# A long convolution fused with a 4-bit gated feed-forward: the last group's kernel tables move from a burst into the first down stage

## The chip, the core and the metric

The kernel runs on one core of a Trainium2 chip. The metric is device time in microseconds (us) of one launch; lower is better. Engines are named as in the profile: PE (TensorE matmul), PEld (its weight loads), DVE (VectorE), ACT (ScalarE), POOL (GpSimd), SP (SyncE, here used only to issue DMAs).

## The reference

`x` is 32 x 64 x 1024 (batch, channel or head, time). Every head is convolved along time with a kernel of 1024 taps made from 64 complex exponentials, and masked by a length for each batch row; the result goes through a feed-forward over the time axis whose weights are 4-bit with a scale and a zero point for each group of 128 rows; `x` is added.

```python
K = 2.0 * einsum('hn,hnl->hl', Cs, exp(P)).real      # P = dtA * arange(L), complex
y = (irfft(rfft(u_m, 2L) * rfft(K, 2L))[..., :L] + u_m * D[:, None]) * mask
gate, up = y2 @ Wg, y2 @ Wu                           # 1024 -> 2752, dequantized in groups of 128
out = x + ((gate * sigmoid(gate) * up) @ Wd)          # 2752 -> 1024
```

## The kernel before

The 64 heads make four blocks of 16 heads; a block is 16 x 32 = 512 columns. The convolution of a head is a product with a Toeplitz matrix: `conv_head` loads it from a padded kernel in DRAM (`t <- kpad`, L525, 512 KB, three buffers `t0`), runs 24 small matmuls (L548) in eight steps of three, and after every second head masks the result on DVE (`y`, L560) and splits it into a high and a low fp16 half (`xh` on ACT, L563; `xl` on POOL, L565). The results of a block fill a pair of tiles `x[b]`, 8 x 512 columns each: blocks 0 and 2 in `x[0]`, blocks 1 and 3 in `x[1]`. The input `u` of four heads is loaded at a time (L503) and split by ACT (L507) and DVE (L510).

The taps of a head's kernel come from tables, made for eight heads at a time: decays (POOL product L175, Exp on ACT L179), phases (DVE L192 to L204), Sin and Square on ACT (L207, L209), factors on DVE (L218 to L223), a small product `kq` on PE (L425, L427), its split `kb` (ACT L430, DVE L431) and two stores to `kpad` (L433). The Toeplitz loads of these heads follow the stores.

The feed-forward runs in chains. A chain has one PSUM buffer and runs over the groups of 128 rows: four matmuls of 512 columns, then one rescale of the PSUM tile by a ratio of scales, on DVE or on ACT, before the next group may add to it. Up chains (`gu_one`, `gu_pair`) have eight groups (matmuls L687, L688; rescales L618 on DVE, L620 on ACT; Silu L695, product L700). Down chains (`dn_pair`) have 21 groups and a rest: matmuls L736 and L737, rescales L637 on DVE and L640 on ACT, the rest `ic` in L741; they end with `o` (L754 DVE or L758 ACT), two additions to the residual `xr` (L762, one on POOL, one on DVE) and two stores. The residual, 512 KB of `x`, is loaded by SP (L775).

The stages, in order, four chains to each down stage:

| stage | chains | beside them |
|---|---|---|
| 0, 1, 2 | up, blocks 0 and 1 | convolution of block 1, unpacking of weights, tables of heads 32 to 47 |
| 3 | down, block 0 | unpacking of down weights (`unpack_it`), `fourth_it`, `convs_it` |
| 4 | down, block 1 | `fourth_it`, `convs_it` |
| 5 | up, blocks 2 and 3 | |
| 6, 7 | down, blocks 2 and 3 | residuals of block 3 |

`fourth` makes the tables of heads 48 to 63 in two groups of eight; `convs` runs the convolution of blocks 2 and 3. `x[0]` and `x[1]` are free from the end of stage 2 until a convolution fills them again.

The order is made by a planner, `roll`. It steps three (in stages 3 and 4) or four open chains in turn, one group each. After each of these steps it makes a *side step*: every side job of the stage gets credit by its rate in `RATES` and runs as many of its own steps as it has credit for. A job with `None` also needs `c.room()`: by the planner's own clocks for PE, DVE and ACT, DVE may be at most 1.2 us ahead of PE and ACT 1.5 us, or it waits; it saves up at most two credits. `convs_it` needs no room. The job marked `True` (`convs_it` in stage 4) is run to its end when the first chain of the next stage opens, which is when the second chain of the stage ends; `c.forced` is set then, and with it all pauses are skipped. A down chain of block 1 follows the last chain of block 0 by two groups or more, since it waits for loads that that chain releases.

The calls become engine queues through the tile framework's scheduler, which takes ready instructions by their place in the program; `with self.after("dve")` ties the instructions inside behind the last rescale issued on that engine.

Unpacking a piece of the weights uses a tile `z` of zero points from a pool `up` with four buffers (`c.up_stack`, right side of SBUF): two loads (L578, L579), a shift on DVE (L584), two additions on POOL that read `z` (L590), two casts on DVE (L599). The steps of the unpacking have pauses for the landing of the loads. Before the change `fourth` waits until all of the down weights are unpacked, closes `up`, and opens a pool `kg2` in that memory for its small tiles. The residual tiles of blocks 0 to 2 share the two buffers of tag `sg` with the Silu results. `convs` forces what is left of the unpacking and of `fourth` between its two blocks:

```python
    def convs():
        yield from c.conv(2)
        c.forced = True
        c.need(*(("dn", k, part) for k in range(4) for part in range(3)))
        every(fourth_it)
        c.forced = False
        yield from c.conv(3)
```

Of the kernel before, what the change touches and what calls it, by code (L numbers as in the profile page):

```python
# [9 lines left out]
F32 = mybir.dt.float32  # L10
# [19 lines left out]
KSCALE = 64.0  # L30
PLACES = {("a", "pair"): 1, ("a", "single"): 2, ("b", "pair"): 3}
MAGIC = 12582912.0
RATES = {"first": (0.5, 4.6), "fill": (1.0, 0.8), "third": 0.5, "convs": 1.9}
HOP, MM, LANDING = 220.0, 215.7, 6000.0
LAG, HEAD_STARTS = 2, [4, 2, 1]
DVE_ROOM, ACT_ROOM = 1200.0, 1500.0
# [190 lines left out]
class Later:  # L227
    def __init__(self, make, *args):
        self.make, self.args, self.gen = make, args, None
# [18 lines left out]
def every(gen):  # L248
    for _ in gen:
        pass  # L250
# [8 lines left out]
class Core:  # L259
    def __init__(self, ctx, tc, io):  # L260
        self.tc, self.nc, self.io = tc, tc.nc, io
        pool = lambda name, **k: ctx.enter_context(tc.tile_pool(name=name, **k))
        self.keep = pool("keep", bufs=1)
        self.cv = pool("cv", bufs=2)
        self.fw = pool("fw", bufs=2)
        self.up_stack = ctx.enter_context(ExitStack())
        self.up = self.up_stack.enter_context(tc.tile_pool(name="up", bufs=4, side="right"))
        self.dram = pool("dram", bufs=1, space=DRAM)
        self.ps, self.ps_stack, self.ps_mode = {}, {}, {}
        for place in "ba":  # L270
            self.ps_stack[place] = ctx.enter_context(ExitStack())
            self.banks(place, "single" if place == "a" else "pair")
        self.tp = self.td = self.ta = 0.0
        self.forced = True
        self.bank_free = {"a": [], "b": []}
        self.kpad = self.dram.tile([H, 2, 1152], F16, name="kpad")
        self.dm, self.known, self.ready = {}, set(), set()
        self.marks = {}
        self.sg, self.t0, self.us, self.raw = {}, {}, {}, {}
        self.passed, self.loaded, self.fac = {}, {}, {}  # L280
        keep = self.keep
        self.w = keep.tile([128, NI, 2, GH, 128], F8, name="w")
        self.wmix = keep.tile([128, GH, 128], F8, name="wmix")
        self.x = [[keep.tile([128, 8, 512], F16, name=f"x{k}{b}") for k in "hl"] for b in range(2)]
        self.ihl = keep.tile([128, 21, 2, 512], F16, name="ihl")
        self.ic = [keep.tile([128, 512], F16, name=f"ic{b}") for b in range(2)]
        self.spill = self.dram.tile([21, 128, 2, 512], F16, name="spill")
        self.zc = self.dram.tile([128, ZBYTES // 128], U8, name="zc")
# [429 lines left out]
    def dn_pair(self, k, blk, place):  # L718
        nc = self.nc
        apart = self.ps_mode[place] == "single"  # L720
        if apart:
            qs = [self.psum("chq", place)[:, 0] for _ in range(2)]
        else:
            q = self.psum("chq", place)
            qs = [q[:, j] for j in range(2)]
        ready = [self.bank(place)] * 2
        for g in range(GI):
            while blk % 2 == 1 and g < 21 and not self.loaded.get((blk, min(20, g + LAG))):
                yield
            if g in (0, 8, 16):  # L730
                self.need(("dn", k, g // 8))
            for j in range(2):
                self.pe((2 if g < 21 else 1) * MM, ready[j])
                lw = self.wd[k][:, g, 128 * j:128 * j + 128]
                if g < 21:
                    nc.tensor.matmul(qs[j], lw, self.ihl[:, g, 0], start=(g == 0), stop=False, skip_group_check=True)  # L736
                    nc.tensor.matmul(qs[j], lw, self.ihl[:, g, 1], start=False, stop=False, skip_group_check=True)  # L737
                    if apart:
                        ready[j] = self.rescale_bank(qs[j], self.rdn[:, 2 * k + j, g:g + 1])
                else:  # L740
                    nc.tensor.matmul(qs[j], lw, self.ic[blk % 2], start=False, stop=True, skip_group_check=True)  # L741
            if g < 21:
                if not apart:
                    ready = [self.rescale_two(q, self.rdn[:, 2 * k:2 * k + 2, g:g + 1])] * 2
                self.passed[blk, g] = self.passed.get((blk, g), 0) + 1
                if blk % 2 == 0 and self.passed[blk, g] == 4:
                    nc.scalar.dma_start(self.ihl[:, g], self.spill[g])
                    self.loaded[blk + 1, g] = True
                yield
        xr = self.res[k] if blk == 3 else self.residual(self.fw, 2 * k, blk)  # L750
        take = self.last_o if blk == 3 else lambda shape, dt: self.fw.tile(shape, dt, name="o", bufs=2)
        o = take([128, 2, 512], F16)
        if not apart and self.on_dve(1240, 1380):
            nc.vector.tensor_tensor(o, q, self.ldn[:, 2 * k:2 * k + 2].unsqueeze(2).to_broadcast([128, 2, 512]), ALU.mult)  # L754
            free = self.dve(1240, self.tp + HOP)
        else:
            for j in range(2):
                nc.scalar.activation(o[:, j], qs[j], AF.Copy, scale=self.ldn[:, 2 * k + j:2 * k + j + 1])  # L758
                free = self.act(690, self.tp + HOP)
        for j in range(2):  # L760
            n = 2 * k + j
            (nc.vector if j == 1 else nc.gpsimd).tensor_tensor(xr[:, j], xr[:, j], o[:, j], ALU.add)  # L762
            if blk < 3:
                store = nc.gpsimd
            else:
                store = nc.scalar if apart and j == 1 else nc.sync
            store.dma_start(self.io["out"][128 * n:128 * n + 128, 512 * blk:512 * blk + 512], xr[:, j])
        self.dve(1000)
        self.bank_free[place].append(free + HOP)
        yield  # L770

    def residual(self, pool, n0, blk):
        rows, cols = slice(128 * n0, 128 * n0 + 256), slice(512 * blk, 512 * blk + 512)
        xr = pool([128, 2, 512], F32) if callable(pool) else pool.tile([128, 2, 512], F32, name="xr", tag="sg", bufs=2)
        self.nc.sync.dma_start(  # L775
            xr, self.io["xT"].rearrange("l h b -> l (h b)")[rows, cols].rearrange("(k p) t -> p k t", p=128))
        return xr
# [65 lines left out]
def tile_ssm_ffn(ctx, tc, io):  # L843
    nc = tc.nc
    c = Core(ctx, tc, io)
# [141 lines left out]
    third_it = third()  # L987
# [13 lines left out]
        return make  # L1001

    def fourth():
        c.forced = True
        every(third_it)
        c.forced = False
        while not c.ready.issuperset(("dn", k, part) for k in range(4) for part in range(3)):
            yield
        c.up_stack.close()
        with tc.tile_pool(name="kg2", bufs=1, side="right") as kg2:  # L1010
            space = c.x[1]
            yield from c.decays(c.scratch(space[:1]), (48, 56))
            c.taps(kg2, 48)
            for h0 in (48, 56):
                yield from c.tables(ScratchPool(c.scratch(space[1:])), h0, 8)
                yield from c.factors(kg2, h0, 8, c.xds[h0])
                for _ in range(3):
                    yield
                c.make_kernel(kg2, h0, 8, "a")
                yield  # L1020

    fourth_it = fourth()

    def convs():
        yield from c.conv(2)
        c.forced = True
        c.need(*(("dn", k, part) for k in range(4) for part in range(3)))
        every(fourth_it)
        c.forced = False
        yield from c.conv(3)  # L1030

    def residuals():
        take = c.scratch(c.x[0])
        c.res = [c.residual(take, n0, 3) for n0 in (0, 2, 4, 6)]
        c.last_o = c.scratch(c.x[1])
        yield

    convs_it = convs()
    second_it = second()
    sides = {  # L1040
        0: [(unpack_it, RATES["first"][0], None), (group_it, 1.0, None), (second_it, RATES["first"][1], True)],
        1: [(unpack_it, RATES["fill"][0], None), (third_it, RATES["fill"][1], None)],
        2: [(third_it, RATES["third"], None), (unpack_it, RATES["fill"][0], None)],
        3: [(unpack_it, RATES["fill"][0], None), (fourth_it, RATES["fill"][1], None), (convs_it, RATES["convs"], False)],
        4: [(fourth_it, RATES["fill"][1], None), (convs_it, RATES["convs"], True)],
        6: [(residuals(), 1.0, True)],
# [80 lines left out]
```

## Time and profile before

| | |
|---|---|
| median of 3 runs | 1074.47 us (1073.33 to 1075.77) |
| the profiled execution | 1075.33 us, its span 1073.5 us |
| PE busy | 1026.2 us, 96% of the span |
| DVE busy | 803.7 us, 75% |
| ACT busy | 775.6 us, 72% |
| POOL busy | 246.5 us, 23% |
| mean granted PE clock | 0.992 |
| down matmuls of stages 3 and 4 | from 395.2 us |
| convolution of block 3 | 510.5 to 580.3 us |

Busy PE time is from modelled ends of pipelined matmuls: it shows where PE waits, not how near it is to its peak. A matmul of 512 columns shows 380 ns but a new one starts every 0.216 us when nothing holds PE. The granted clock is the share of full speed that PE was given; it is read beside the idle time, since matmuls at half clock still count as busy.

### The profile page before, as it was taken

How to read it: one execution, taken by the hardware profiler on the slowest of the kernel's cores; microseconds unless marked ns; L12 is line 12 of the kernel's file. 1: busy time of each engine (PE TensorE's matmuls, PEld its weight loads, DVE VectorE, ACT ScalarE, POOL GpSimd, SP SyncE). 2: the span in 40 equal slices, each digit the busy share in tenths (PEclk: the TensorE clock that was granted, in tenths of full speed). 3: DMA queues.
4: the chain of work that ended last, by engine and by line, in shares of the span. 5: the costliest groups of instructions: out<-in, count | busy, mean ns of one | idle time of the engine just before them, and what ended most of it. 6: DMA issues, size and time to landing. Idle time of an engine off the chain costs nothing.

```text
span 1073.5 us, 15382 instructions
## 1 busy us (share of the span) xinstructions
PE 1026.2 (96%) x5854; PEld 513.5 (48%) x5854; DVE 803.7 (75%) x939; ACT 775.6 (72%) x1034; POOL 246.5 (23%) x270
## 2 busy tenths in 40 slices
PE   3989999999999999997999999999999999999996
PEld 2867444444344445663665444444444444444442
DVE  8965788888977786768446777777877777777776
ACT  5767777787677777777577777666666667878775
POOL 0333233232332242231103112221111222102102
PEclk9999999999999999999999999999999999999998
DMA  6976321111111534546753001000000001424102
GB/s 197 331 244 211 101 69 40 40 59 40 42 48 50 143 88 156 164 156 196 231 167 128 30 29 51 20 13 17 20 20 20 20 20 58 129 79 148 59 1 79
DMA packets 52099, 99.76 MB, mean 93 GB/s; under 512 B 9524, under 2 KB 11444, under 8 KB 52024
## 3 DMA queue, kind: packets, MB, share of 16 engines
q1 hardware_dynamic: 38888, 70.09, 20.8%
q0 software_dynamic: 5280, 17.31, 4.3%
q10 hardware_dynamic: 7856, 11.37, 3.6%
q8 instruction: 46, 0.75, 0.3%
q14 instruction: 29, 0.24, 0.1%
HBM read 78.99 MB, written 19.76 MB: 92 GB/s over the span
## 4 chain that ended last, share of the span: by engine, by line
PE 83%; ACT 5%; DMA 4%; DVE 4%; issue 2%; POOL 0%; SPq 0%; DVEq 0%; ACTq 0%
PE chq L687 23%; PE chq L688 22%; PE chq L736 13%; PE chq L737 13%; PE cq L548 6%; PE chq L664 2%; PE chq L665 2%; DMA t<-kpad 2%; ACT chq L640 1%; DVE chq L618 1%; ACT chq L620 1%; DVE v L700 1%; DMA ihl<-kpad 1%; DMA ihl<-xF 1%; PE chq L741 1%
## 5 line engine op out<-in xcount | busy, mean ns | idle before, releaser
L687 PE MATMUL chq<-xh,w 128*128 128x512 f16 x1216 | 460.4, 380 | 5.7 <-DVE chq L618 2.1
L688 PE MATMUL chq<-xl,w 128*128 128x512 f16 x1216 | 458.6, 380 | 0.0
L618 DVE TENSOR_SCALAR chq<-chq,gur 128x1024 f32<-128x1024 f32 x261 | 333.2, 1289 | 95.3 <-PE chq L688 94.1
L620 ACT ACTIVATE chq<-chq,gur 128x1024 f32<-128x1024 f32 x285 | 304.3, 1085 | 86.8 <-PE chq L688 85.5
L640 ACT ACTIVATE chq<-chq,dnr 128x512 f32<-128x512 f32 x372 | 242.1, 661 | 71.7 <-PE chq L737 63.8
L736 PE MATMUL chq<-ihl,wd 128*128 128x512 f16 x672 | 253.8, 380 | 6.5 <-ACT chq L640 3.5
L737 PE MATMUL chq<-ihl,wd 128*128 128x512 f16 x672 | 253.4, 380 | 0.0
L637 DVE TENSOR_TENSOR chq<-chq,dnr 128x1024 f32<-128x1024 f32 x129 | 158.4, 1231 | 83.6 <-PE chq L737 83.2
L688 PEld LDWEIGHTS <-w 128*128 128x128 fp8e4 x1216 | 118.9, 98 | 155.3 <-issue 19.4
L687 PEld LDWEIGHTS <-w 128*128 128x128 fp8e4 x1216 | 118.9, 98 | 145.9 <-issue 1.9
L310 POOL TENSOR_TENSOR ihl<-v,ihl 128x512 f16<-128x512 f32 x42 | 48.3, 1150 | 362.9 <-ACT ihl L629 362.9
L737 PEld LDWEIGHTS <-wd 128*128 128x128 fp8e4 x672 | 65.5, 98 | 76.0 <-issue 12.7
L548 PEld LDWEIGHTS <-t 128*128 128x128 f16 x1152 | 81.4, 98 | 39.2 <-DMA t<-kpad 5.9
L736 PEld LDWEIGHTS <-wd 128*128 128x128 fp8e4 x672 | 65.7, 98 | 67.7 <-issue 1.7
L548 PE MATMUL cq<-uh,t 128*128 128x256 f16 (+3 forms) x720 | 91.8, 226 | 4.6 <-DMA t<-kpad 4.5
L565 POOL TENSOR_TENSOR xl<-y,xh 128x512 f16<-128x512 f32 x28 | 36.2, 1294 | 161.5 <-ACT xh L563 161.5
L548 PE MATMUL cq<-ul,t 128*128 128x256 f16 (+3 forms) x360 | 71.6, 225 | 0.0
L629 ACT CAST ihl<-v 128x512 f16<-128x512 f32 x42 | 25.9, 617 | 58.7 <-DVE v L700 55.3
L700 DVE SCALAR_TENSOR_TENSOR v<-chq,gul,sg 128x1024 f32<-128x1024 f32 x38 | 48.6, 1280 | 17.1 <-PE chq L688 11.3
L310 POOL TENSOR_TENSOR spill<-v,spill 128x512 f16<-128x512 f32 x42 | 48.8, 1161 | 14.2 <-ACT spill L629 13.9
L640 ACT ACTIVATE chq<-chq,gur 128x512 f32<-128x512 f32 x66 | 43.2, 661 | 11.0 <-PE chq L665 9.8
L590 POOL TENSOR_TENSOR w<-w,z 128x256 int32<-128x256 int32 x42 | 31.5, 770 | 82.0 <-DVE w L584 77.6
(250 smaller groups left out, 820.5 us busy)
## 6 DMA issues: line engine op xcount, KB each, us to landing
t<-kpad SPq DMA_DIRECT2D x48, 512.0 KB, 4.4
spill<-spill POOLq DMA_DIRECT2D x42, 256.0 KB, 2.7
ihl<-spill ACTq DMA_DIRECT2D x42, 256.0 KB, 2.8
z<-zc SPq DMA_DIRECT2D x29, 256.0 KB, 3.7
u<-xF SPq DMA_DIRECT2D x12, 512.0 KB, 3.7
xr<-xT SPq DMA_DIRECT2D x12, 512.0 KB, 4.7
out<-xr POOLq DMA_DIRECT2D x24, 256.0 KB, 2.9
w<-qgu SPq DMA_DIRECT2D x21, 256.0 KB, 4.1
```

Of the source, the lines that this page charges most:

```text
L310: self.nc.gpsimd.tensor_tensor(out, a, b, op)
L548: nc.tensor.matmul(q[:, d:, h % 2, :], t0[:, lw, 128 * d:128 * d + 128], uu[:, 0:8 - d, h % 4, :], start=(d == 0 and k == 0 and h % 2 == 0 ...
L565: split.tensor_tensor(xl[:, :, ts], yv, xh[:, :, ts], ALU.subtract)
L618: self.mark("dve", self.nc.vector.tensor_scalar(q, q, col, None, ALU.mult))
L620: self.mark("act", self.nc.scalar.activation(q, q, AF.Copy, scale=col))
L637: self.mark("dve", self.nc.vector.tensor_tensor(q, q, cols.to_broadcast([128, 2, 512]), ALU.mult))
L640: self.mark("act", self.nc.scalar.activation(q[:, k], q[:, k], AF.Copy, scale=cols[:, k]))
L687: nc.tensor.matmul(q[:, b], lw, xh[:, g, :], start=(g == 0), stop=False, skip_group_check=True)
L688: nc.tensor.matmul(q[:, b], lw, xl[:, g, :], start=False, stop=(g == GH - 1), skip_group_check=True)
L700: nc.vector.scalar_tensor_tensor(v, q, last, self.sg.pop(ct - 21), ALU.mult, ALU.mult)
L736: nc.tensor.matmul(qs[j], lw, self.ihl[:, g, 0], start=(g == 0), stop=False, skip_group_check=True)
L737: nc.tensor.matmul(qs[j], lw, self.ihl[:, g, 1], start=False, stop=False, skip_group_check=True)
```

## The change

- `fourth` no longer waits for the unpacking, and no longer uses `kg2`. From the start of stage 3 it takes all of its memory from `x[1]`: decays in the first half of the high tile, the dpad row, factors and `kb` in the rest of it and the last eighth of the low tile, phase tables in the other seven eighths.
- Between the factors and `make_kernel` it pauses until the planner's PE clock has reached its DVE clock, in place of three steps.
- `convs` no longer forces anything between its blocks. If heads 56 to 63 are not known it lets its steps pass; only when it is itself run to the end does it run `fourth` on.
- The rate of `convs` goes from 1.9 to 1.52 steps for each side step.
- The residuals of blocks 0 to 2 get a pool `xrp` of two buffers in the memory of `up`. The first down chain to end forces what is left of the unpacking, closes `up` and opens `xrp`.

```diff
-RATES = {"first": (0.5, 4.6), "fill": (1.0, 0.8), "third": 0.5, "convs": 1.9}
+RATES = {"first": (0.5, 4.6), "fill": (1.0, 0.8), "third": 0.5, "convs": 1.52}
...
-        xr = self.res[k] if blk == 3 else self.residual(self.fw, 2 * k, blk)
+        if blk == 3:
+            xr = self.res[k]
+        else:
+            if self.xrp is None:
+                self.need(*(("dn", j, part) for j in range(4) for part in range(3)))
+                self.up_stack.close()
+                self.xrp = self.up_stack.enter_context(self.tc.tile_pool(name="xrp", bufs=2, side="right"))
+            xr = self.residual(self.xrp, 2 * k, blk)
...
-        xr = pool([128, 2, 512], F32) if callable(pool) else pool.tile([128, 2, 512], F32, name="xr", tag="sg", bufs=2)
+        xr = pool([128, 2, 512], F32) if callable(pool) else pool.tile([128, 2, 512], F32, name="xr")
...
     def fourth():
-        c.forced = True
-        every(third_it)
-        c.forced = False
-        while not c.ready.issuperset(("dn", k, part) for k in range(4) for part in range(3)):
+        first, second = c.x[1]
+        yield from c.decays(c.scratch([first[:, :4]]), (48, 56))
+        c.taps(ScratchPool(c.scratch([first[:, 4:6]])), 48)
+        for h0 in (48, 56):
+            small = ScratchPool(c.scratch([first[:, 6:8], second[:, 7:8]]))
+            yield from c.tables(ScratchPool(c.scratch([second[:, :7]])), h0, 8)
+            yield from c.factors(small, h0, 8, c.xds[h0])
+            yield from c.pause(c.td - c.tp + HOP)
+            c.make_kernel(small, h0, 8, "a")
             yield
-        c.up_stack.close()
-        with tc.tile_pool(name="kg2", bufs=1, side="right") as kg2:
-            space = c.x[1]
-            yield from c.decays(c.scratch(space[:1]), (48, 56))
-            c.taps(kg2, 48)
-            for h0 in (48, 56):
-                yield from c.tables(ScratchPool(c.scratch(space[1:])), h0, 8)
-                yield from c.factors(kg2, h0, 8, c.xds[h0])
-                for _ in range(3):
-                    yield
-                c.make_kernel(kg2, h0, 8, "a")
-                yield
...
     def convs():
         yield from c.conv(2)
-        c.forced = True
-        c.need(*(("dn", k, part) for k in range(4) for part in range(3)))
-        every(fourth_it)
-        c.forced = False
+        while 56 not in c.known:
+            if c.forced:
+                next(fourth_it)
+            yield
         yield from c.conv(3)
```

More of the change, by code (lines that the diff above doesn't have):

```diff
@@ L276, in __init__ @@
         self.kpad = self.dram.tile([H, 2, 1152], F16, name="kpad")
+        self.xrp = None
         self.dm, self.known, self.ready = {}, set(), set()
```

## The prediction, made before the changed kernel ran

> **What bounds the kernel now.** I read the page's forty slices first, then the windows of 10 us, then inside the weak stretch the chain of waits and PE's timeline.
>
> ```profile
> PE   3989999999999999997999999999999999999996
> PEclk9999999999999999999999999999999999999998
> ```
>
> One slice is 26.8 us. PE is full from the fourth slice to the last but one, with a single "7", at 483 to 510 us. Whatever does not touch PE's gaps there moves little. The windows show the hole (columns: stretch, length, busy us of PE, PEld, DVE, ACT, POOL with counts, granted clock, DMA share, GB/s):
>
> ```profile
> 480.00:490.00 10.00, 9.99 (x74) 5.33 (x73) 8.23 (x10) 7.10 (x10) 6.24 (x7) 1.00 0.78 266
> 490.00:500.00 10.00, 6.36 (x36) 2.74 (x35) 9.85 (x21) 7.08 (x12) 0.00 (x0) 0.86 0.54 178
> 500.00:510.00 10.00, 7.25 (x43) 2.97 (x42) 7.33 (x12) 7.80 (x16) 0.00 (x0) 0.97 0.56 156
> 510.00:520.00 10.00, 8.53 (x98) 6.75 (x99) 1.31 (x3) 3.21 (x6) 1.15 (x1) 1.00 0.92 297
> 520.00:530.00 10.00, 10.00 (x79) 6.04 (x78) 6.44 (x6) 7.07 (x11) 1.16 (x1) 1.00 0.51 161
> 497.00:500.00 3.00, 3.00 (x23) 1.43 (x22) 3.00 (x7) 1.22 (x2) 0.00 (x0) 0.53 0.31 87
> ```
>
> PE idles 3.64 + 2.75 + 1.47 us; DVE has 21 instructions in the first of the three; from 497 to 500 us the clock is 0.53. The chain of waits says what PE waited for (start, length, what):
>
> ```profile
> 491.24 1.24 ACT chq L640 x2
> 492.50 1.28 ACT L207
> 493.79 0.94 ACT xl L207 x2
> 494.73 0.82 ACT xl L209 x2
> 495.55 1.14 ACT chq L640 x2
> ...
> 504.58 5.92 DMA t<-kpad
> 510.55 1.71 PE cq L548 x24
> 512.27 4.72 DMA t<-kpad
> ```
>
> First a down chain's rescale (L640) stands behind the sine tables (L207, L209) of the last group of heads, all issued in one burst. Then the first Toeplitz loads (t<-kpad) of block 3 start only when that burst has written its kernel to DRAM.
>
> How much is lost: from 484 to 518 us PE ran 34 matmuls each on L736 and L737, at the unhindered spacing of 0.216 us: 14.7 us. The convolution pieces in the chain and timeline add up to 6.1 us (three heads from 510.55 to 515.39, and ends), the kq matmuls to 2.7 us. That is 23.5 us of work in 34 us: **10.5 us lost**, 7.9 of it idle, some 1.4 (3.0 x 0.47) half clock, the rest small seams.
>
> A page differs on the clock: by the Trainium skill, "TensorE: Matmul & The Clock Gate", section "What's actually happening", the clock halves only after about 3.4 us idle. The longest gap here was 2.21 us, so by that rule 1.4 us less would be recoverable; the row decides.
>
> **The change, part by part.**
>
> *The burst becomes a side job (saves up to 10.5 us).* The last group's tables no longer wait for the last unpacking and are no longer forced in one go. The instructions stay the same. On DVE a group has 14 (L192 0.68, L194 0.68, L197 0.48, L198 0.34, L200 0.68, L201 0.41, L203 0.74, L204 0.47, five of about 0.41 in L218 to L223, L431 0.41): 7.0 us, two groups 13.9 us. On ACT: two table loads of 1.28, Exp 1.06, sines and squares 1.86 and 2.02, two kb of 0.37: 8.2 us. They go into the stretch 406 to 484 us, where DVE was busy 52.1 of 78 us and ACT 57.9. Each goes to about 66 of 78, 85%; with the slower convolution pace the same chain work takes some 74 us, so near 90%. That cover is thin. The nearest row is the same job done earlier for heads 32 to 47 inside the up stage:
>
> ```profile
> 220.00:230.00 10.00, 9.78 (x45) 4.28 (x44) 7.32 (x7) 9.69 (x11) 4.77 (x6) 1.00 0.18 66
> 230.00:240.00 10.00, 9.51 (x44) 4.13 (x43) 10.00 (x15) 7.30 (x10) 1.95 (x3) 1.00 0.29 79
> 240.00:250.00 10.00, 9.83 (x47) 4.33 (x46) 9.77 (x10) 5.46 (x7) 0.92 (x1) 1.00 0.00 0
> 250.00:260.00 10.00, 9.19 (x42) 3.90 (x41) 7.75 (x11) 8.15 (x10) 5.21 (x6) 1.00 0.15 55
> 280.00:290.00 10.00, 8.00 (x29) 3.00 (x28) 9.39 (x10) 4.81 (x6) 6.58 (x8) 0.83 0.15 54
> ```
>
> There PE lost 1.7 us over 40 us, and once, at 280 us, 2.0 idle plus 1.7 (10 x 0.17) of clock. Bounds 0 to 5.4 us; I take 2.0, next to the 1.7.
>
> The two table switches now delay rescales in a stage that needs ACT. In the trace a switch costs its 1.28 us and the next ACTIVATE starts 0.01 us later (492.50 to 493.79). "ScalarE: Activation LUTs", section "What ACT_TABLE_LOAD costs", in the Trainium skill speaks against the move: it counts a drain too, 2.66 us a switch. By it ACT would have 2.8 us more; no such drain shows here.
>
> Of what else moves with it: the dpad load and the four kpad stores (16 KB) pass on SP ahead of Toeplitz loads of block 2. Two of them held SP 2.25 us at 508.72; those loads are issued up to three heads (about 14 us) ahead, so 0. The two POOL multiplies of the decays were already hoisted to 385 and 392 us and waited there 7.6 us for the up stage; they write the same half of the same block: 0. Behind them on POOL stand only unpacking adds.
>
> *The convolution pace, 1.9 to 1.52.* Blocks 2 and 3 are 32 heads of 8 steps, 256. Stage 5 opens when the second chain of stage 4 ends, its last matmul at 576.17 us, and what remains is drained at once:
>
> ```profile
> 576.00:582.00 6.00, 2.45 (x33) 2.10 (x32) 1.00 0.09 35
> ```
>
> That is L548 alone: 33 matmuls, 11 steps left; 245 were done, so 245 / 1.9 = 129 side steps. At 1.52 they give 196: **60 steps, 7.5 heads, will be drained in one block** at stage 5's door. PE's work is the same, and the first five sixths of stages 3 and 4 get shorter by what is put off. What a block costs is the wait for Toeplitz loads: three buffers, a load issued at 512.27 landed 4.72 us later, while two further heads last 3.2 us. At 515.39 this left 1.65 us, half filled by chain matmuls: PE idled 0.84. Behind the first three heads come 4.5 more, 1.5 such gaps, 2.5 us unfilled, 1.3 at that filling. Two chains of stage 4 are at hand to fill. Bounds 0 to 4.5 (unfilled, with one half-clock stretch of 2 us); I take 1.5.
>
> Whether the tables are ready in time: block 2 needs 128 / 1.52 = 84 side steps. The new generator takes about 5 + 3 steps for the decays and 16 for each group (pauses counted at 1.1 us a step), 40 in all; at rate 0.8 that is 50 side steps if DVE and ACT have room, and there are 84 before block 3 would wait and 129 before stage 5.
>
> *Residuals in the unpacking's memory.* Two buffers as before, but loads for the first two chains can't start at 400 us any more; they wait for the last POOL add of the unpacking (465.7 us). Chain ends were at 472.0 and 478.9, a load lands in about 4.7 us: just in time, as the third chain's was already (issued 480.86, added 484.77, no wait). If late, DVE would hold rescales behind its add (L762). Bounds 0 to 2 x 4.7; I take 0.5. The forced end of the unpacking pulls forward at most three DVE instructions (0.41 + 0.68 + 0.78), which ended at 472.4 anyway: 0, at worst 1.9. In stage 5 and 6 silu tiles no longer share buffers with residuals; the seam at 640 us (9.91 of 10) says 0.1 at most.
>
> **Sum.** 10.5 - 2.0 - 1.5 - 0.5 = 6.5 us. The profiled execution took 1075.33 us (span 1073.5), the median of the runs is 1074.47, 0.9 below; from the median: **1068.0 us**. With all costs at 0 it is 1064.0; with 7 us of costs 1071.
>
> **Rivals.**
>
> *The gain is eaten (same).* Near 90% load in stage 3, a late residual and a bad drain cost 8.4 to 12.6 together (5.4 + 4.5 + 1 is 10.9). For it: DVE at 10.0 did cost PE half a microsecond in 10. Against: all would have to lie near their upper ends. About 1074.
>
> *The burst comes back at stage 5's door (slower).* Tables go ahead only when DVE and ACT have room, and at 85 to 90% they may be refused. If heads 56 to 63 are not known after 129 side steps, the rest of the tables is forced there and the whole of block 3 follows as a block: the 10.5 us stay, 16 heads at a load rhythm of 2.15 us ((4.72 + 1.7) / 3) instead of 1.6 add 8.8, half filled: 4 to 9 us, about 1080. It decides at 0.31 table steps per side step (40 / 129). Between 84 and 129 side steps block 3 only starts late and the drain grows. Against: a quarter of both engines was idle in 406 to 484 us.
>
> *It doesn't take effect.* If the table instructions keep a late place on their engines, the hole remains and only the pace changes: 1074 to 1077. The steps are tied behind the rescales current when they are issued, so I give this little.
>
> **How the numbers follow.** Forecast with its own range 1064 to 1071.5: 0.70. Eaten or no effect: 0.18, of which 0.03 is still faster by over 0.2% and 0.03 slower. Burst at the door, or costs past the bounds: 0.12. About 0.2% (2.1 us) is what a measurement of this kernel can tell from no change. Hence faster 0.73, within 0.12, slower 0.15. For 8 in 10 the range takes in the forecast and the rival about 1074: 1063.5 to 1076.5.
>
> **What would show it.** Right: Sin and Square of the last group between 415 and 480 us and PE over 9.7 in each window of 10 us there; no window under 9 at 480 to 520; the first Toeplitz load of block 3 ahead of the last head of block 2; 150 to 200 L548 matmuls behind the second ic matmuls of stage 4 (now 33). Wrong: PE below 9.5 in several windows of stage 3 (the cover is too thin), DVE waiting for xr, PE waiting for t<-kpad by over 3 us in the drain, or the last kb behind stage 4's second chain.

## The result, and the profile after

The changed kernel takes 1079.51 us (median of 6 runs, 1078.84 to 1081.79) against 1075.06 for the kernel before on the same chip: ratio 1.0048, 95% interval 1.0036 to 1.0060. It is half a per cent slower; 1068.0 and a range of 1063.5 to 1076.5 had been forecast. The profiled execution took 1081.79 us, the longest of the six; its span is 1080.0.

In the changed kernel the lines have moved, by one from `self.xrp = None` on and by eight behind the new pool in `dn_pair`: the convolution is L549, its Toeplitz load L526, the down rescales L638 and L641, the down matmuls L737 and L738, `ic` L742, the residual's additions L770, its load L783.

The windows of 10 us (columns as before: PE, PEld, DVE, ACT, POOL, granted clock, DMA share, GB/s):

```profile
460.00:470.00 10.00, 9.19 (x74) 5.32 (x71) 7.01 (x10) 7.07 (x12) 2.10 (x3) 1.00 0.47 149
...
480.00:490.00 10.00, 8.16 (x70) 5.09 (x69) 8.31 (x11) 5.64 (x9) 6.87 (x7) 1.00 0.75 260
490.00:500.00 10.00, 9.29 (x56) 5.19 (x56) 8.08 (x10) 5.98 (x11) 1.05 (x2) 0.83 0.97 306
500.00:510.00 10.00, 9.30 (x71) 5.15 (x69) 7.95 (x9) 5.06 (x9) 0.12 (x1) 1.00 0.59 201
510.00:520.00 10.00, 10.00 (x63) 4.81 (x62) 5.63 (x8) 7.45 (x14) 0.00 (x0) 1.00 0.45 136
...
570.00:580.00 10.00, 3.40 (x33) 2.23 (x34) 2.39 (x3) 2.46 (x4) 2.79 (x4) 0.86 0.82 259
580.00:590.00 10.00, 10.00 (x105) 8.18 (x104) 1.41 (x3) 1.94 (x3) 1.16 (x1) 0.80 0.47 171
```

The hole at 490 to 520 us, where PE had lost 7.9 us idle, is down to 1.4. Smaller gaps have come ahead of it, from 460 on (0.81 and 1.84 us in the windows at 460 and 480), and a new hole stands at 570 to 580: PE idles 6.6 us and runs the next 10 us at 0.80 of its clock. That is the door of stage 5, where the rest of block 3 is drained. L549 alone there:

```profile
563.50:592.00 28.50, 15.10 (x195) 14.04 (x195) 0.88 0.62 198
```

195 matmuls are 65 steps, eight heads; before there were 33. What PE waited for, from its timeline (the bracket is the idle time and its releaser):

```profile
571.39 0.28 PE L549 MATMUL cq<-uh,t 128*128 128x256 f16 x1 [1.43 <-DMA t<-kpad]
...
579.81 0.40 PE L549 MATMUL cq<-uh,t 128*128 128x256 f16 x1 [5.20 <-DMA t<-kpad]
```

SP's timeline, and from its waits at 540 to 600 us (us in total, times, longest) what its residual loads waited for:

```profile
560.35 6.94 SPq L526 DMA_DIRECT2D t<-kpad  x3
573.14 0.37 SPq L783 DMA_DIRECT2D xr<-xT  x1
573.61 2.34 SPq L526 DMA_DIRECT2D t<-kpad  x3
...
SPq L783 <- DMA out<-xr: 11.8, 3, 6.1
```

Between 567.3 and 573.1 us SP issues nothing, then one residual load, and only behind it three Toeplitz loads, the first of which PE gets at 579.8. PE had done with the three heads before by 569.8, so Toeplitz buffers were free. SP issues in order here: the residual load needs a buffer whose store has landed, and while it waits nothing behind it starts.

The chain of waits shows the gaps of stage 3:

```profile
471.33 1.44 POOL wd L591 x2
472.78 3.81 DMA xr<-xT
476.75 1.63 POOL xr L770
...
478.67 0.45 POOL out L775
479.22 2.63 DMA out<-xr
...
482.00 4.79 DMA xr<-xT
...
486.92 0.69 DVE xr L770
487.62 1.56 DVE xl L200
...
489.51 1.15 DVE chq L638
```

The first residual is loaded at 472.78, since the unpacking frees its memory only then (its last additions, L591, end at 472.77), though its chain's last matmul was at 470.2. Its store frees the buffer for the third residual at 482.0. The third addition (L770) holds DVE for that load, two table instructions follow (L200, L201), and then the rescale that PE awaits: 2.55 us idle at 490.7.

### The profile page after: what moved, and what is told of

It reads as the page before. It is cut to its first block, busy times and chain, and to the rows that moved or that the text cites. A ratio compares the mean times of both kernels' runs of the same rounds, so it can differ in the third digit from the quotient of the medians.

```text
span 1080.0 us, 15399 instructions
## 1 busy us (share of the span) xinstructions
PE 1026.8 (95%) x5854; PEld 513.8 (48%) x5854; DVE 812.7 (75%) x943; ACT 769.2 (71%) x1026; POOL 247.8 (23%) x270
## 4 chain that ended last, share of the span: by engine, by line
PE 79%; DVE 7%; DMA 6%; ACT 5%; issue 2%; POOL 1%; SPq 0%; DVEq 0%; POOLq 0%; ACTq 0%
PE chq L688 22%; PE chq L689 22%; PE chq L737 12%; PE chq L738 12%; PE cq L549 5%; PE chq L665 2%; PE chq L666 2%; DMA t<-kpad 2%; ACT chq L641 2%; DVE chq L619 1%; DMA kpad<-kb 1%; DVE v L701 1%; ACT chq L621 1%; DMA xr<-xT 1%; DMA w<-kpad 1%
## 5 line engine op out<-in xcount | busy, mean ns | idle before, releaser
L641 ACT ACTIVATE chq<-chq,dnr 128x512 f32<-128x512 f32 x362 | 235.3, 661 | 74.7 <-PE chq L738 68.0
L737 PE MATMUL chq<-ihl,wd 128*128 128x512 f16 x672 | 253.2, 380 | 5.8 <-DVE chq L638 3.2
L738 PE MATMUL chq<-ihl,wd 128*128 128x512 f16 x672 | 252.3, 380 | 0.0
L638 DVE TENSOR_TENSOR chq<-chq,dnr 128x1024 f32<-128x1024 f32 x134 | 163.6, 1230 | 74.5 <-PE chq L738 72.5
L549 PEld LDWEIGHTS <-t 128*128 128x128 f16 x1152 | 82.9, 100 | 41.9 <-DMA t<-kpad 10.8
L549 PE MATMUL cq<-uh,t 128*128 128x256 f16 (+3 forms) x720 | 92.7, 231 | 10.2 <-DMA t<-kpad 10.2
L738 PEld LDWEIGHTS <-wd 128*128 128x128 fp8e4 x672 | 65.6, 98 | 76.6 <-issue 10.8
L737 PEld LDWEIGHTS <-wd 128*128 128x128 fp8e4 x672 | 65.4, 98 | 69.2 <-DVE wd L600 1.6
L549 PE MATMUL cq<-ul,t 128*128 128x256 f16 (+3 forms) x360 | 73.2, 230 | 0.0
L641 ACT ACTIVATE chq<-chq,gur 128x512 f32<-128x512 f32 x66 | 43.3, 661 | 14.9 <-PE chq L666 13.8
L591 POOL TENSOR_TENSOR w<-w,z 128x256 int32<-128x256 int32 x42 | 31.6, 771 | 81.1 <-DVE w L585 80.3
```

Of the source, the lines that this page charges most:

```text
L549: nc.tensor.matmul(q[:, d:, h % 2, :], t0[:, lw, 128 * d:128 * d + 128], uu[:, 0:8 - d, h % 4, :], start=(d == 0 and k == 0 and h % 2 == 0 ...
L638: self.mark("dve", self.nc.vector.tensor_tensor(q, q, cols.to_broadcast([128, 2, 512]), ALU.mult))
L641: self.mark("act", self.nc.scalar.activation(q[:, k], q[:, k], AF.Copy, scale=cols[:, k]))
```

## The experiments

All times are medians; each ratio is to the kernel before, run on the same chip. The rows come from several chips, on which the kernel before took 1074.6 to 1076.0 us, so two rows are best compared by their ratios.

| run | us | ratio (95%) |
|---|---|---|
| changed kernel | 1079.5 | 1.0036 to 1.0060 |
| xr_behind_t | 1077.5 | 1.0011 to 1.0032 |
| old_residuals | 1079.6 | 1.0029 to 1.0054 |
| fast_block3 | 1071.3 | 0.9945 to 0.9974 |
| before_152 | 1078.8 | 1.0024 to 1.0051 |
| t0_four | 1080.3 | 1.0026 to 1.0061 |
| t0_four_xr_behind_t | 1074.7 | 0.9977 to 1.0006 |
| pace_19_only | 1072.9 | 0.9965 to 0.9984 |
| xr_four_fast_block3 | 1069.2 | 0.9925 to 0.9958 |
| pace_19_fast_block3 | 1067.2 | 0.9909 to 0.9940 |
| pace_19_fast_xr_four | 1068.0 | 0.9916 to 0.9945 |
| pace_19_fast_old_residuals | 1068.2 | 0.9910 to 0.9947 |

**xr_behind_t.** Is it the residual in SP's queue?

```diff
-        self.nc.sync.dma_start(xr, ...)
+        with self.after("sp" if blk == 1 else None):
+            self.nc.sync.dma_start(xr, ...)
```

> The changed kernel (1079.5), but the residual loads of block 1 (stage 4) are tied behind the last Toeplitz or input load issued by then, so that no residual load that waits for a buffer stands ahead of drained Toeplitz loads on SP. Theory 1 (SP's queue: at 573.14 us a residual load that had waited for a store let three Toeplitz loads go only at 573.6): the 5.2 us wait of PE before 579.8 and about 2 us of half clock behind it go, 1072 to 1074. Theory 2 (three Toeplitz buffers are too few for heads in a block, whatever the order): 1078 to 1080. Theory 3 (tables beside the down stage overload DVE and ACT): no change, 1079.5.

1077.5: 2.0 us less than the changed kernel (2.8 by the ratios), not 6. The wait of 5.2 us is gone, but others have come in its place:

```profile
571.18 0.28 PE L549 MATMUL cq<-uh,t 128*128 128x256 f16 x1 [1.68 <-DMA t<-kpad]
574.38 0.28 PE L549 MATMUL cq<-uh,t 128*128 128x256 f16 x1 [1.50 <-DMA t<-kpad]
577.38 0.28 PE L549 MATMUL cq<-uh,t 128*128 128x256 f16 x1 [1.31 <-DMA t<-kpad]
581.21 0.28 PE L549 MATMUL cq<-uh,t 128*128 128x256 f16 x1 [0.37 <-DMA t<-kpad]
```

These add up to 4.9 us, with the clock at full speed this time. Theory 1 explains less than half of what the drain costs; something else holds the loads behind it. The DMA engines are 98% busy from 570 to 580 us (329 GB/s), so three buffers are not the only candidate.

**old_residuals.** `xr` back in tag `sg`, with no forced unpacking and no `xrp`.

> The changed kernel with the residuals back in the two buffers of tag sg; the tables stay in x[1] and the pace at 1.52. Theory 1 (the residuals' new place is the cause: it delays the first three residuals, which cost PE 2.55 + 0.7 + 0.8 us idle and about 1.7 us of clock at 467 to 503 us, and it puts a waiting load among the drained Toeplitz loads): both go, 12 us less, 1067 to 1069. Theory 2 (three Toeplitz buffers): only the first part goes, 1074 to 1075. Theory 3 (tables overload DVE and ACT): 1078 to 1080.

1079.6: no difference, the number of the third expectation, though PE does not wait for tables. In the drain it waits 4.4 us in four pieces, like xr_behind_t. What that and the first residuals gave was lost again in stage 3: on SP a residual load waited for a store until 489.3, and a Toeplitz load behind it came late (3.48 us of PE's time). A spill load, which ACT issues, cost 1.68 us more; it took 8.16 us to land, and why was not traced. SP waits for residual stores here too, 19.2 us from 455 to 600, against 26.2 in the changed kernel.

**fast_block3.** Nothing left to drain.

```diff
-        yield from c.conv(3)
+        for n, _ in enumerate(c.conv(3)):
+            if n % 2:
+                yield
```

> The changed kernel, but the convolution of block 3 takes two of its steps for each step of convs, so that it ends before the second chain of stage 4 and nothing is left to drain; the residuals as changed. Theories 1 and 2 (the drain costs 6.6 us idle and about 2 us of clock): 1070 to 1072. Theory 3 (tables): 1078 to 1080. If the faster pace makes PE wait for Toeplitz loads within stage 4 instead: 1074 or more.

1071.3, as expected: 8.2 us less than the changed kernel (9.6 by the ratios), and without the drain the change is faster than before. PE has no wait over 0.2 us from 510 to 605 us; stage 3 keeps its gaps (0.76, 1.81 and 0.70 us). The edit acts on block 3 alone, but the two profiled executions (spans 1080.0 and 1069.2) differ in stage 3 too: the gap at 490 us is 2.55 in one and 1.81 in the other, and only the first was followed by a lower clock (0.83 for 10 us, 1.7 us). The drain itself costs 8.6 us in that profile, 6.6 idle and 2.0 of clock.

**before_152.** The pace alone, in the kernel before.

> The kernel before with the rate of convs at 1.52 and nothing else changed: the burst stays, six and a half heads are drained at the door of stage 5, and in its SP order no residual load stands between the drained Toeplitz loads. Theory 1 (SP's queue): about as before, 1075 to 1077. Theory 2 (three Toeplitz buffers): the drain costs 7 to 9 us here too, 1082 to 1084. Theory 3 says nothing of it (1075).

1078.8, between the two theories: 4 us slower than before. In its drain PE waits 1.15 and 3.15 us for `t <- kpad`, at a clock of 0.91 to 0.92. It also shows the 0.76 us at 466 us for the last unpacking, which the kernel before has not: a slower convolution brings the chains' ends forward, the unpacking keeps its pauses. And it shows the gap behind the third residual, with the residuals in `sg` and no table instruction on DVE before 491.9:

```profile
483.77 0.69 DVE L762 TENSOR_TENSOR xr<-xr,o 128x512 f32<-128x512 f32 x1 [2.12 <-DMA xr<-xT]
...
485.66 0.38 PE L736 MATMUL chq<-ihl,wd 128*128 128x512 f16 x1 [1.77 <-DVE chq L637]
```

So that gap comes with the slower pace, not with the new pool alone. The burst costs less here: from 490 to 520 us PE idles 2.7 us in place of 7.9. At 1.9 there is no convolution matmul from 490 to 510 us, here there are 63; that they fill the burst's hole is likely, but no run tries it alone.

**t0_four.** Four Toeplitz buffers (`bufs=4`, loads asked for four heads ahead).

> The changed kernel with four Toeplitz buffers in place of three and loads asked for four heads ahead, from head 32 on; pace 1.52, the drain of seven heads and the residuals as changed. Theory 2 (a drained head takes a third of a load's round trip, (4.75 + 1.7) / 3 = 2.15 us, against 1.6 us on PE): with four buffers the round trip is 1.61 us a head, the 4.4 to 4.9 us that PE waited in the drain of the runs without the residual in SP's way go for the most part, and what the residual adds stays: 1074.5 to 1076.5. Theory 1 alone (only the residual in SP's queue counts): 1078 to 1080.

1080.3, no gain in the whole time. The first wait fell from 1.43 to 0.35 us; the second stayed, and SP's timeline says why:

```profile
573.32 0.37 SPq L783 DMA_DIRECT2D xr<-xT  x1
573.80 1.43 SPq L526 DMA_DIRECT2D t<-kpad  x3
```

The residual load comes at the same time as in the changed kernel, again with three Toeplitz loads behind it. The whole time does not show the drain alone: in stage 3 this profile has a gap of 3.54 us at 489.8, with the clock at 0.94 and then 0.72 for 10 us each, against 2.55 and 0.83 in the changed kernel.

**t0_four_xr_behind_t.** Both edits.

> The changed kernel with both edits to the drain: four Toeplitz buffers, and the residual loads of block 1 behind the Toeplitz loads on SP. Alone the first left a wait of 5.5 us on SP's blocked loads, and the second left 4.9 us of rhythm. If the two limits lie one behind the other: with both, PE waits 1 us or less in the drain, 1072 to 1074. If a drained block is slow for a third reason (the masks and splits between heads, or DMA bandwidth): 1076 or more.

1074.7: 5.6 us less than t0_four and 2.8 less than xr_behind_t, between the two expectations. The fourth buffer gains only when the residual is out of SP's way: two limits, one behind the other, are shown, though PE still waits 3.0 us and not 1. Two waits are left, 1.53 and 1.46 us, and the window points at a third:

```profile
570.00:580.00 10.00, 6.93 (x109) 6.49 (x106) 1.65 (x3) 1.85 (x3) 3.42 (x3) 1.00 0.93 331
```

The DMA engines are 93% busy. At 331 GB/s a load of 512 KB lasts 1.6 us, as long as its head on PE; with four buffers the median landing is 6.1 us (5.1 with three, in xr_behind_t). That bandwidth is this last limit is read from the window, not tried by itself; the share was as high with three buffers.

**pace_19_only.** The rate alone undone.

> The changed kernel with the rate of convs back at 1.9 and nothing else: by the code five heads are drained in place of seven, and the chains of stage 3 end later against the unpacking and the residuals. If the pace in stage 3 counts (3.2 us of PE's waits at 468 to 502 us and 1.7 us of clock go with it) and the drain of five heads costs 3 to 6 us: 1071 to 1075. If only the drain counts, by heads (5/7 of 8 us): 1077 to 1078.

1072.9, 0.25% faster than before: with its old rate the change gains. All gaps of stage 3 from 460 us on are gone (no wait of PE over 0.4 us up to 560). The first residual is now loaded at 468.4, ahead of its chain's end. The drain of five heads still costs waits of 1.21, 0.55 and 4.01 us, with a clock of 0.83 from 570 to 580.

**xr_four_fast_block3.** Four residual buffers on top of fast_block3.

> Fast_block3 (1071.3) with four residual buffers in the pool xrp in place of two, so that no residual load of stage 3 waits for a store. Theory 1 (the chain load, add, store, load, add of the first and the third residual holds DVE and so PE, 1.81 + 0.70 us at 490 and 500 us): 2.5 us less, 1068.5 to 1069.5. Theory 3 (that time belongs to the tables, which are queued on DVE there): 1071 to 1072.

1069.2, 2.1 us less than fast_block3 by the medians, but the intervals overlap. In the traces the wait on DVE at 490 us falls from 1.81 to 1.15, that at 500 is gone (a spill load costs 0.48). Net of the spill load that is 0.9 us. Some of that time belongs to the residuals, and the 1.15 that stay to the tables, behind which the rescale is queued on a DVE that is busy throughout; the split is suggested, not shown.

**pace_19_fast_block3.** The old rate and no drain.

> Fast_block3 with the rate of convs back at 1.9; block 3 then takes 3.8 steps for each side step once its kernel is known and is done well ahead of stage 5's door. If the slower pace costs time in stage 3 (chain ends come before the last unpacking, 0.76 us at 468 us in every kernel at 1.52): 1070 to 1071. If the convolution only has to be spread and not drained: 1071 to 1072. If the doubled pace makes PE wait for Toeplitz loads (a head every 3.2 us against 2.15 us for a load): over 1073.

1067.2, better than all three expectations, 0.76% faster than before and the best version here, 4.1 us below fast_block3 (3.8 by the ratios). All that PE waits for from 395 to 600 us:

```profile
PE chq L688 <- ACT chq L621: 1.3, 3, 0.5
PE chq L737 <- ACT chq L641: 0.4, 2, 0.2
PE cq L549 <- DVE y L561: 0.4, 1, 0.4
PE chq L737 <- ACT sg L696: 0.2, 1, 0.2
```

2.3 us, for the tables and all else (the kernel before has 0.8 of them too, at 400 to 411 us), with DVE 10.00 of 10 us busy at 480 to 490.

**pace_19_fast_xr_four and pace_19_fast_old_residuals.** The same with four residual buffers, and with the residuals in `sg`.

> Pace_19_fast_block3 with four residual buffers, so that residual loads wait for no store. In that kernel PE waits only 2.3 us in all from 400 to 600 us, none of it on a residual: 1066.5 to 1067.5, no difference to be measured. If SP's waits for residual buffers still delay other loads: 1065 to 1066.

> Pace_19_fast_block3 (1067.2) with the residuals back in tag sg. If the tables' early place is what gains and the residuals' new pool gains nothing: 1066.5 to 1068. If the pool is needed: 1069 or more.

1068.0 and 1068.2: neither differs from 1067.2 beyond the noise. At the old rate without a drain the residuals' place is worth nothing that these runs could measure, though in `sg` a spill load costs PE 1.36 us. What gains is the tables' early place, together with block 3's convolution spread over stage 4.

## Why the prediction was wrong

**The burst: right.** The hole was where the forecast saw it, and it goes when the tables move. At the same rate of 1.9 all of PE's waits at 490 to 520 us are gone in pace_19_only. pace_19_fast_block3 gains 8.2 us (0.76% of 1075), of the 10.5 less 2.0 forecast for this part. What the burst costs hangs on the pace, though: in before_152 PE idles only 2.7 us beside it.

**The tables' cover: right at the old rate.** 2.0 us taken; 2.3 us of waits are left in pace_19_fast_block3, all causes together. The forecast's sign of a thin cover, PE below 9.5 in several windows of stage 3, did come in the changed kernel (9.19, 8.16, 9.29, 9.30). It came with the pace: at 1.9 the windows from 460 to 520 are 9.94 or more (pace_19_only) with the tables in the same place. At 1.52 tables queued on DVE keep part of it, 1.15 us in xr_four_fast_block3. In the changed kernel the switch to Sin at 441.62 us took 1.28 us and the next ACTIVATE came 0.02 us later, so the row held. The drain that the Trainium skill counts with each switch ("ScalarE: Activation LUTs", section "What ACT_TABLE_LOAD costs") did not show here.

**How much would be drained: right.** 60 steps forecast, 65 measured.

**What the drain costs: the step that failed.** Taken 1.5 us, bounds 0 to 4.5. In the profile it costs 8.6 (6.6 idle, 2.0 of clock), and fast_block3 is 8.2 us faster without it (9.6 by the ratios, stage 3 included): outside the bounds. The price came from a single gap at 515 us, half filled with chain matmuls, with no residual load on SP. Three things differed. Little filled: in the changed kernel 96 convolution matmuls (four heads) stand in a row on PE from 565.2 us, with the first wait before the last head, and between its two waits PE had, beside that head, just seven chain matmuls; a chain that is open but queued behind the block is no cover. A residual load stood among the Toeplitz loads on SP, waiting for a store. And the loads themselves are slower when asked for at PE's pace: with the residual moved away and three buffers they land in 5.1 us (median, xr_behind_t), with four buffers in 6.1, where the forecast took 4.72. The forecast followed SP's queue for the kpad stores and not for the residual loads, which have two buffers that come free late.

**The residuals: mis-sized.** Taken 0.5, "just in time", with the last addition of the unpacking at 465.7 us as in the kernel before; in the changed kernel it ended at 472.8. So they were late, DVE held rescales behind its addition as the forecast had feared, and 2.55 and 0.70 us of idle time and a clock of 0.83 for 10 us (1.7 us) followed. The cost lay inside the bounds of 0 to 9.4.

**The pace in stage 3: left out.** The rate was costed as a drain alone. It also shortens stage 3 against what is paced by time, the unpacking and with it the residuals' memory; the two rates differ by 3.8 us without any drain (0.9959 for fast_block3, 0.9924 for pace_19_fast_block3). The gaps at 466 and 486 us in before_152 say the same for the kernel before.

The terms by the ratios: 8.2 us gained by the tables' move (10.5 less 2.3), 3.8 lost by the pace and the residuals in stage 3, 9.6 lost by the drain, the longer gap in stage 3 included: 5.2 slower, which is the ratio of 1.0048. The last two are steps from one kernel to the next, so the sum closes by itself and tests nothing; the test is the 8.2. One number, 1.52 for 1.9, is the whole difference between the loss (1.0048) and the gain of pace_19_only (0.9975); a rate that doubles for block 3 makes it 0.9924.

**The rivals.** The loss did not come as the slower rival had it: the last stores of the tables' kernels were issued at 519.1 us, long before stage 5's door at 563. What came is the small case of costs past the bounds. Part of the rival's second half, heads drained at the rhythm of their loads, is in it, at eight heads in place of sixteen and with little filling; the larger wait, 5.2 us, was SP's blocked queue.

## What to carry to other kernels

When filler work is put off, look where its remainder is forced out, and price it there with nothing beside it: by the in-order queue of the issuing engine (is there a DMA ahead that waits for a buffer?), then by buffers, then by bandwidth; one limit removed only uncovers the next. A pace is tied to everything that runs by time beside it, so a change that moves work must have its rate set anew. Buffers that come free just in time in the old trace may be late in the new one, and on an in-order queue they hold up what stands behind them.

## What the runs showed of the hardware

The clock did not fall behind single gaps of 1.81 us (fast_block3) or of 1.68, 1.50 and 1.31 us close together (xr_behind_t); it fell to 0.83 for 10 us behind 2.55 us and to 0.80 behind 5.20 us (changed kernel), and to 0.53 from 497 to 500 us behind 2.21 us with 0.91 and 0.52 us close by (kernel before). The Trainium skill ("TensorE: Matmul & The Clock Gate", section "What's actually happening") names an idle window of about 3.4 us for the fall; here 2.55 us alone, and 2.21 us with the two shorter gaps, were enough.
